# Where and when a mixture-of-experts kernel loads its router's logits, and the order of work around it

## The chip, the cores and the metric

The kernel runs on one core of a Trainium2 chip. The metric is the device time of one execution in microseconds; smaller is better. Times before: 385.84 us as the median of three runs (385.48 to 386.31). A core has TensorE (PE; matmuls, with its weight loads listed apart as PEld), VectorE (DVE), ScalarE (ACT), GpSimd (POOL) and SyncE (SP, which here only issues DMAs). TensorE writes its products to PSUM banks; the other data lie in SBUF. The engines run in parallel and wait for each other by semaphores; each engine takes its own instructions strictly in the order in which they were written.

## The reference

Two layers with residual connections, on x of shape (2, 1024, 256), with a condition of shape (2, 8):

```
rw = softmax(cond);  w, sel = top_k(rw, 2);  w = w / sum(w)          # two experts for each of the 2 batch rows
mlp(x, g, u, d) = (gelu_tanh(x @ g) * (x @ u)) @ d                   # 256 -> 1024 -> 256
x = x + sum_{s in sel} w_s * mlp(x, expert_s) + mlp(x, shared)       # 8 experts, one shared MLP
x = x + (x @ W_base.T + b_base + 2.0 * sum_e cond_e * (x @ A_e.T) @ B_e.T)
```

Of the 8 experts only the two chosen ones count for a batch row, so the kernel loads the weights of these two alone, by an index that it works out on the chip. For that it needs the 16 numbers of `cond_8` (the logits).

## The kernel before, in words

The work is cut into 24 groups: 2 batch rows, for each the shared MLP and two experts, for each 4 quarters of the 1024 inner columns (256 columns in two blocks of 128). `groups` at L185 lists them; groups 0 to 3 and 12 to 15 are the shared MLP's. A group's weights are one tile `w_raw` of 128 x 1536 numbers (768 KB): four blocks of the gate and up weights, A11, A12, A22, A21, and the down weights. Three such tiles turn round (`raw_ring`). Shared weights are loaded by SP; group 0's come in four pieces, between the four tiles of x (`load_first`, `load_x`). An expert's weights are gathered by GpSimd (`load_w`, L200), which needs the indices `idx`.

To keep float32 accuracy every operand is split into a high and a low part (`hi_of`, L179, and `lo_of`, L182), and a product of two blocks is three matmuls (high by high, low by high, high by low). The high parts are mostly made by ScalarE, the low parts by VectorE or GpSimd. A block in what follows is three matmuls of 128x128 by 128x512.

From group 1 on, the four 2 x 2 block products of the gate (g) and of the up weights (u) are computed by a scheme with seven products each, P1 to P7, in place of eight, with sums of the weight blocks (`weight_sum`, S1 to S4, made by GpSimd at L221 into `sf`) and of x (`x_sum`). The products gather in two PSUM banks for g and two for u, called a and d. In between, ScalarE copies what bank a holds to SBUF (`keep`, L310: r1 after P1, u2 after P6, u3 after P7), and VectorE adds that to bank d (`add_part`, L316: "r1 added", "u3 added", "u2 added"). The results are the four parts 00, 11, 10 and 01 of the hidden layer. Each then goes through gelu on ScalarE (L325), a product with the up part on VectorE (`times_up`, L331 and L333, "act 00" and so on), and a split into high and low part ("hi 00" on ScalarE, "lo 00" on VectorE). Then come six matmuls with the down weights into the banks y (L355), as two halves; the second half needs the low part. Group 0 does the same with eight plain products (`plain_product`, L306).

TensorE's order inside a group is thus a list of 14 blocks of products and 8 half-blocks of "down", 22 in all. All of it, for all engines, is one list: `at(t, f, ...)` at L106 puts a step with a due time t into `plan`, in units of about one block of TensorE, and L618 calls the steps in order of their due times. What a group repeats has its due time within the group in the table `REGULAR`, and group g adds g x 22 (`LEN`). `MOVED` shifts single steps by their number in the list. So a table of numbers sets the order in which each engine gets its instructions; nothing is reordered later. The waits follow from the data.

The parts that this change touches:

- `router_load` (L148) loads the logits to all 128 partitions (8 KB) and makes the row numbers by an iota on GpSimd. Its due time of 14.5 is shifted by `MOVED[11]` to -33.0, so it is the first step of all.
- `router` (L152, due 26) finds the two largest logits and the indices on VectorE. `gate_exp` and `gelu_table` (due 48.0 and 48.1, in group 2) run an exponential on ScalarE and then set the table for gelu again; `gate_weights` (due 52.5, L169 to L171) makes the experts' weights on VectorE. They are first used in group 4.
- SP's order at the start is: piece 0 of group 0's weights, x tile P1, piece 1, x tile P2, piece 2, x tiles B12 and P3, piece 3, the weights of group 1, of group 2, of group 3, the second layer's weights.

Of the kernel before, what the change touches and what calls it, by code (L numbers as in the profile page):

```python
# [50 lines left out]
P = 128  # L51
# [2 lines left out]
SCALING = 2.0  # L54
PIECE = 2
REGULAR = {
    "P1g": -3.3, "r1g": -2.5, "P2g": -0.5, "S1": -0.4, "A hi": -0.0, "P1u": 0.1, "r1u": 0.2,
    "r1 added g": 0.8, "P6g": 1.9, "u2g": 2.6, "P2u": 3.4, "gelu 00": 4.5, "P5g": 5.3, "S2": 5.5, "S4": 6.5,
    "P6u": 7.2, "load": 7.2, "S3": 7.9, "P7g": 8.4, "u2u": 8.7, "P5g mix": 9.0, "u3g": 9.7, "P7u": 11.3,
    "S hi": 12.0, "r1 added u": 12.1, "P5u": 12.2, "u3 added g": 12.7, "act 00": 12.7, "A1 lo": 13.4,  # L60
    "S lo": 13.5, "P4g": 13.8, "u3u": 14.1, "hi 00": 15.2, "gelu 11": 15.3, "P3g": 15.5, "u3 added u": 15.6,
    "act 11": 16.6, "gelu 10": 17.8, "P4u": 17.8, "u2 added g": 18.2, "P3u": 18.5, "hi 11": 19.4,
    "act 10": 19.7, "hi 10": 19.8, "lo 00": 20.7, "gelu 01": 21.2, "down 00 0": 21.3, "u2 added u": 21.7,
    "act 01": 22.9, "lo 11": 23.6, "down 00 1": 24.2, "A2 lo": 28.6, "hi 01": 29.5, "lo 10": 30.6,
    "down 11 0": 32.5, "down 11 1": 32.5, "down 10 0": 32.8, "D hi": 33.0, "lo 01": 33.2, "down 10 1": 33.3,
    "down 01 0": 34.0, "down 01 1": 35.1, "D1 lo": 36.1, "D0 lo": 36.3,
}
MOVED = {
    11: -47.5, 39: 2.3, 53: 0.6, 66: -0.2, 80: -1.0, 86: -11.0, 99: 7.4, 100: 6.6, 120: -2.6, 1577: 6.8,
    1580: 2.9, 1583: 6.7, 1604: 7.1,  # L70
}
WARM = 32
LEN = 22
# [15 lines left out]
def moe_then_lora(ctx: ExitStack, tc: tile.TileContext, x, cond, skill, shared, piece0, second, outT):  # L89

    nc = tc.nc
    B, T, NC, _, _ = x.shape
    E = cond.shape[1]
# [12 lines left out]
    def at(t, f, *args):  # L106
        plan.append((round(t + MOVED.get(len(plan), 0), 1), len(plan), f, args))
# [6 lines left out]
    def const(shape, dtype, name):  # L114
        return sb.tile(shape, dtype, name=name, tag=name)
# [22 lines left out]
    logits = const([P, B, E], F32, "logits")  # L138
# [7 lines left out]
    gate_w = const([P, TOP_K, B], F32, "gate_w")  # L146

    def router_load():  # L148
        nc.gpsimd.dma_start(out=logits, in_=bass.AP(cond.tensor, 0, [[0, P], [E, B], [1, E]]))
        nc.gpsimd.iota(row, pattern=[[1, NPC]], base=0, channel_multiplier=NPC)  # L150

    def router():  # L152
# [159 lines left out]
    sums, ge, act, acts = {}, {}, {}, {}  # L312
# [49 lines left out]
    mix, bias_sb = lin[:, (2 + NC) * C:(2 + NC) * C + B], lin[:, (2 + NC) * C + B:]  # L362
# [70 lines left out]
    V, A, G = nc.vector, nc.scalar, nc.gpsimd  # L433
# [8 lines left out]
    at(-29.4, load_x, 0, 1, 1)  # L442
    at(-29.3, load_first, 4 * G2, PW)
    at(-29.2, load_w, 1)
    at(14.5, router_load)
    at(17, load_w, 2)
    at(40, load_lora)

# [238 lines left out]
```

## Time and profile before

| What | us |
|---|---|
| median of three runs | 385.84 |
| the profiled execution, its own time | 386.39 |
| its span | 384.6 |
| one group of TensorE in the steady part (two runs of twelve down matmuls of the chain, 102.16 and 117.12) | 14.96 |
| TensorE busy in the first 10 us | 7.03 |
| TensorE busy from 40 to 50 us | 9.00 |
| VectorE busy from 155 to 170 us (about group 10) | 14.68 |
| VectorE busy from 245 to 260 us | 12.97 |
| GpSimd busy from 155 to 170 us | 9.44 |

The profile has a page of one execution and a trace that can be asked for more. In its lists a line of a wait reads: engine and line that waited, who released it, the sum, the times, the longest. A line of the order of time reads: start, duration, engine, line, operation, what is written and read. The granted TensorE clock is full over the whole span. All times inside the span are from its start. The names are the program's: `ps_ag` is bank a for the gate, `ps_du` bank d for the up weights, `acts` the split hidden parts, `xr` the loaded x tiles, `x` their split parts.

### The profile page before, as it was taken

How to read it: one execution, taken by the hardware profiler on the slowest of the kernel's cores; microseconds unless marked ns; L12 is line 12 of the kernel's file. 1: busy time of each engine (PE TensorE's matmuls, PEld its weight loads, DVE VectorE, ACT ScalarE, POOL GpSimd, SP SyncE). 2: the span in 40 equal slices, each digit the busy share in tenths (PEclk: the TensorE clock that was granted, in tenths of full speed). 3: DMA queues.
4: the chain of work that ended last, by engine and by line, in shares of the span. 5: the costliest groups of instructions: out<-in, count | busy, mean ns of one | idle time of the engine just before them, and what ended most of it. 6: DMA issues, size and time to landing. Idle time of an engine off the chain costs nothing.

```text
span 384.6 us, 4819 instructions
## 1 busy us (share of the span) xinstructions
PE 377.3 (98%) x1694; PEld 312.5 (81%) x1694; DVE 330.7 (86%) x421; ACT 250.8 (65%) x439; POOL 214.8 (56%) x216
## 2 busy tenths in 40 slices
PE   6999899999999999999999999999999999999996
PEld 5888788888888888888888888888888888888885
DVE  4999898697988999999989999889889889787586
ACT  3688786775775867757658767757667566575520
POOL 1676687689675574564463765755755745650100
PEclk9999999999999999999999999999999999999999
DMA  7611221120220213030342202202202112000014
GB/s 232 262 55 55 83 84 14 70 80 2 84 82 0 84 43 120 3 136 27 111 125 66 84 0 82 83 2 82 77 7 82 34 50 82 0 2 1 0 56 164
DMA packets 7831, 26.00 MB, mean 68 GB/s; under 512 B 880, under 2 KB 1664, under 8 KB 7808
## 3 DMA queue, kind: packets, MB, share of 16 engines
q0 software_dynamic: 2336, 12.59, 10.5%
q1 hardware_dynamic: 5472, 13.11, 9.9%
q8 instruction: 13, 0.21, 0.2%
q14 instruction: 10, 0.08, 0.1%
HBM read 23.60 MB, written 2.10 MB: 67 GB/s over the span
## 4 chain that ended last, share of the span: by engine, by line
PE 95%; ACT 2%; DMA 1%; DVE 1%; SPq 0%; issue 0%
PE y L355 33%; PE ps_au L286 17%; PE ps_ag L286 17%; PE ps_du L286 13%; PE ps_dg L286 13%; DMA xr<-in_x 1%; PE ps_dg L306 1%; PE ps_du L306 1%; PE ps_ag L306 1%; PE ps_au L306 1%; DVE gate_w L171 0%; PE ps_dg L378 0%; ACT L175 0%; ACT L165 0%; SPq L209 0%; ACT wa L179 0%
## 5 line engine op out<-in xcount | busy, mean ns | idle before, releaser
L355 PE MATMUL y<-acts,wd 128*128 128x512 f32 x576 | 149.9, 389 | 1.0 <-DVE acts L182 1.0
L355 PEld LDWEIGHTS y<-acts,wd 128*128 128x128 f32 x576 | 108.0, 188 | 23.8 <-DVE acts L182 1.4
L182 DVE TENSOR_TENSOR acts<-act,acts 128x512 fp32r<-128x512 f32 x96 | 90.5, 970 | 1.1 <-ACT acts L179 0.9
L182 POOL TENSOR_TENSOR wd<-w_raw,wd 128x256 fp32r<-128x256 f32 x44 | 41.9, 975 | 68.8 <-ACT wd L179 68.8
L182 POOL TENSOR_TENSOR wa<-w_raw,wa 128x512 fp32r<-128x512 f32 (+1 forms) x46 | 55.7, 1212 | 23.6 <-ACT wa L179 23.6
L179 ACT CAST acts<-act 128x512 fp32r<-128x512 f32 x96 | 59.6, 621 | 10.5 <-DVE act L331 6.4
L221 POOL TENSOR_TENSOR sf<-w_raw 128x256 f32<-128x256 f32 x46 | 44.6, 970 | 37.5 <-DVE ws L182 27.4
L310 ACT COPY u_u<-ps_au 128x512 f32<-128x512 f32 x46 | 27.1, 589 | 48.2 <-PE ps_au L286 48.1
L333 DVE SCALAR_TENSOR_TENSOR act<-ge,gate_w,c_u 128x512 f32<-128x512 f32 x48 | 46.4, 966 | 1.9 <-ACT ge L325 0.4
L316 DVE TENSOR_TENSOR c_u<-ps_du,u_u 128x512 f32<-128x512 f32 x46 | 31.4, 684 | 15.6 <-PE ps_du L286 12.8
L325 ACT ACTIVATE ge<-c_g 128x512 f32<-128x512 f32 x69 | 44.0, 638 | 0.0
L316 DVE TENSOR_TENSOR c_g<-ps_dg,u_g 128x512 f32<-128x512 f32 x46 | 31.6, 686 | 13.5 <-PE ps_dg L286 7.4
L286 PE MATMUL ps_au<-x,ws 128*128 128x512 f32 x138 | 38.8, 389 | 0.0
L286 PE MATMUL ps_ag<-x,ws 128*128 128x512 f32 x138 | 38.8, 389 | 0.0
L286 PE MATMUL ps_dg<-x,ws 128*128 128x512 f32 x138 | 38.8, 389 | 0.0
L286 PE MATMUL ps_du<-x,ws 128*128 128x512 f32 x138 | 38.8, 389 | 0.0
L286 PE MATMUL ps_ag<-x,wa 128*128 128x512 f32 x138 | 38.8, 389 | 0.0
L286 PE MATMUL ps_au<-x,wa 128*128 128x512 f32 x138 | 38.8, 389 | 0.0
L182 DVE TENSOR_TENSOR ws<-sf,ws 128x1024 fp32r<-128x1024 f32 (+1 forms) x24 | 37.2, 1552 | 0.0
L310 ACT COPY r_g<-ps_ag 128x512 f32<-128x512 f32 x23 | 13.5, 589 | 29.5 <-PE ps_ag L286 29.4
L286 PEld LDWEIGHTS ps_ag<-x,ws 128*128 128x128 f32 x138 | 25.9, 188 | 5.4
L286 PEld LDWEIGHTS ps_dg<-x,ws 128*128 128x128 f32 x138 | 25.9, 188 | 5.4
(102 smaller groups left out, 554.0 us busy)
## 6 DMA issues: line engine op xcount, KB each, us to landing
w_raw<-in_shared SPq DMA_DIRECT2D x7, 768.0 KB, 4.5
xr<-in_x SPq DMA_DIRECT2D x16, 256.0 KB, 2.9
lora_in<-in_second SPq DMA_DIRECT2D x1, 514.0 KB, 5.3
w_raw<-in_piece SPq DMA_DIRECT2D x2, 256.0 KB, 5.7
outT<-u_g SPq DMA_DIRECT2D x2, 256.0 KB, 2.0
outT<-u_u SPq DMA_DIRECT2D x2, 256.0 KB, 2.0
outT<-ge SPq DMA_DIRECT2D x4, 128.0 KB, 1.7
w_raw<-in_piece SPq DMA_DIRECT2D x2, 128.0 KB, 3.2
```

Source lines behind the costliest of these rows:

```text
L179: (eng.copy if eng is nc.scalar else eng.tensor_copy)(pair[:, 0, :], src)
L182: eng.tensor_tensor(pair[:, 1, :], src, pair[:, 0, :].bitcast(F32), ALU.subtract)
L221: eng.tensor_tensor(ssum(i), a, b, op)
L286: nc.tensor.matmul(ps, lhsT=l, rhs=r, start=(start and n == 0), stop=(n == len(parts) - 1), skip_group_check=True)
L306: nc.tensor.matmul(bank[plain_bank[ij], h], lhsT=w[:, wp, c:c + P], rhs=x[:, xp, :], start=(k == 0 and n == 0), stop=(n == 2), skip_group_ ...
L310: nc.scalar.copy(part[m, h], bank["a", h])
L316: nc.vector.tensor_tensor(sums[g, h, ij], bank["d", h], part[m, h], ALU.add)
L325: nc.scalar.activation(ge[g, ij], result(g, 0, ij), AF.Gelu_apprx_tanh)
L333: nc.vector.scalar_tensor_tensor(act[g, ij], ge[g, ij], gate_w[:, s - 1, b:b + 1], result(g, 1, ij), ALU.mult, ALU.mult)
L355: nc.tensor.matmul(y[j][c], lhsT=w[:, wp, o:o + P], rhs=a[:, ap, :], start=first and n == 0, stop=last and n == 2, skip_group_check=True)
```

## The change

The load of the logits is issued by SP, not by GpSimd, and its due time is -29.1: behind the weights of group 1 (-29.2) and ahead of those of group 2 (17). The iota stays on GpSimd. All due times in `REGULAR` are new, and so are the shifts in `MOVED`. For single steps: `x_sum(0,1)` (number 32) is done on VectorE between the high and the low part of x tile B12 and not behind the low part of group 0's down weights; the high part of P5 (40) goes ahead of group 0's gelu 10 on ScalarE; GpSimd's S3 of group 1 (86) keeps its place as GpSimd's first sum; gelu 11 of group 0 (74) goes ahead of the weight sums' split.

In the groups the order by due time changes as follows. Place 0 is P1g.

| place | TensorE before | TensorE after |
|---|---|---|
| 0 to 5 | P1g, down 00 first half, P2g, P1u, P6g, down 00 second half | the same |
| 6 to 9 | P2u, P5g, P6u, P7g | down 11 first half, P6u, P2u, P7g |
| 10 to 13 | down 11 first and second half, down 10 both halves | P5g, down 10 both halves, down 11 second half |
| 14 to 17 | P7u, down 01 first half, P5u, down 01 second half | the same |
| 18 to 21 | P4g, P3g, P4u, P3u | P3g, P4g, P4u, P3u |

On ScalarE "hi 10" moves from ahead of gelu 01 to behind the copy u2g, and the high part of the down weights and of the weight sums stand a little earlier. On VectorE "lo 10" goes ahead of "lo 11" (in groups 1 to 22); in group 2's stretch both stand ahead of `gate_weights`, where before `lo 10` stood behind it. On GpSimd, S3 goes ahead of the low part of A22 and of the gather, and the two low parts of the down weights change places.

```diff
--- before.py
+++ after.py
@@ -54,20 +54,20 @@
 SCALING = 2.0
 PIECE = 2
 REGULAR = {
-    "P1g": -3.3, "r1g": -2.5, "P2g": -0.5, "S1": -0.4, "A hi": -0.0, "P1u": 0.1, "r1u": 0.2,
-    "r1 added g": 0.8, "P6g": 1.9, "u2g": 2.6, "P2u": 3.4, "gelu 00": 4.5, "P5g": 5.3, "S2": 5.5, "S4": 6.5,
-    "P6u": 7.2, "load": 7.2, "S3": 7.9, "P7g": 8.4, "u2u": 8.7, "P5g mix": 9.0, "u3g": 9.7, "P7u": 11.3,
-    "S hi": 12.0, "r1 added u": 12.1, "P5u": 12.2, "u3 added g": 12.7, "act 00": 12.7, "A1 lo": 13.4,
-    "S lo": 13.5, "P4g": 13.8, "u3u": 14.1, "hi 00": 15.2, "gelu 11": 15.3, "P3g": 15.5, "u3 added u": 15.6,
-    "act 11": 16.6, "gelu 10": 17.8, "P4u": 17.8, "u2 added g": 18.2, "P3u": 18.5, "hi 11": 19.4,
-    "act 10": 19.7, "hi 10": 19.8, "lo 00": 20.7, "gelu 01": 21.2, "down 00 0": 21.3, "u2 added u": 21.7,
-    "act 01": 22.9, "lo 11": 23.6, "down 00 1": 24.2, "A2 lo": 28.6, "hi 01": 29.5, "lo 10": 30.6,
-    "down 11 0": 32.5, "down 11 1": 32.5, "down 10 0": 32.8, "D hi": 33.0, "lo 01": 33.2, "down 10 1": 33.3,
-    "down 01 0": 34.0, "down 01 1": 35.1, "D1 lo": 36.1, "D0 lo": 36.3,
+    "P1g": -2.2, "r1g": -1.4, "P2g": -1.3, "S1": -0.3, "A hi": -0.0, "r1 added g": 0.2, "P1u": 0.7,
+    "r1u": 0.7, "P6g": 1.7, "u2g": 2.1, "P6u": 4.6, "gelu 00": 5.2, "S2": 6.8, "S4": 6.8, "S3": 7.1,
+    "P2u": 7.4, "load": 7.4, "P7g": 7.8, "P5g mix": 8.6, "P5g": 8.7, "u2u": 8.8, "P7u": 10.2, "u3g": 10.6,
+    "S hi": 10.7, "r1 added u": 11.6, "A1 lo": 12.1, "u3 added g": 12.7, "act 00": 12.9, "P5u": 12.9,
+    "S lo": 14.3, "P3g": 14.4, "u3u": 14.5, "P4g": 14.9, "u3 added u": 16.2, "gelu 11": 16.3, "hi 00": 16.4,
+    "P4u": 16.4, "gelu 10": 16.7, "act 11": 16.8, "P3u": 17.8, "u2 added g": 18.0, "act 10": 18.6,
+    "hi 11": 19.6, "down 00 0": 20.3, "lo 00": 20.8, "gelu 01": 21.6, "u2 added u": 21.6, "act 01": 23.4,
+    "down 00 1": 25.0, "hi 10": 25.3, "down 11 0": 25.8, "lo 10": 28.4, "hi 01": 29.2, "A2 lo": 30.0,
+    "lo 11": 30.2, "down 10 0": 30.8, "down 10 1": 31.4, "down 11 1": 31.5, "D hi": 32.7, "lo 01": 32.9,
+    "down 01 0": 34.1, "down 01 1": 35.8, "D0 lo": 36.9, "D1 lo": 37.4,
 }
 MOVED = {
-    11: -47.5, 39: 2.3, 53: 0.6, 66: -0.2, 80: -1.0, 86: -11.0, 99: 7.4, 100: 6.6, 120: -2.6, 1577: 6.8,
-    1580: 2.9, 1583: 6.7, 1604: 7.1,
+    32: -9.6, 39: 0.8, 40: -5.4, 53: 0.9, 74: -2.1, 80: -1.3, 86: -42.5, 99: 7.1, 100: 6.3, 1514: -5.7,
+    1536: 3.7, 1577: 7.7, 1580: 3.3, 1583: 7.5, 1604: 8.8,
 }
 WARM = 32
 LEN = 22
@@ -146,7 +146,7 @@
     gate_w = const([P, TOP_K, B], F32, "gate_w")
 
     def router_load():
-        nc.gpsimd.dma_start(out=logits, in_=bass.AP(cond.tensor, 0, [[0, P], [E, B], [1, E]]))
+        nc.sync.dma_start(out=logits, in_=bass.AP(cond.tensor, 0, [[0, P], [E, B], [1, E]]))
         nc.gpsimd.iota(row, pattern=[[1, NPC]], base=0, channel_multiplier=NPC)
 
     def router():
@@ -442,7 +442,7 @@
     at(-29.4, load_x, 0, 1, 1)
     at(-29.3, load_first, 4 * G2, PW)
     at(-29.2, load_w, 1)
-    at(14.5, router_load)
+    at(-29.1, router_load)
     at(17, load_w, 2)
     at(40, load_lora)
```

## The prediction, made before the result was known

> **What bounds the kernel now.** I read the page first, then TensorE's waits, then the chain of work, then the first 8 us and the stretch from 36 to 43 us closely.
>
> ```profile
> PE 377.3 (98%) x1694; PEld 312.5 (81%) x1694; DVE 330.7 (86%) x421; ACT 250.8 (65%) x439; POOL 214.8 (56%) x216
> ...
> PE 95%; ACT 2%; DMA 1%; DVE 1%; SPq 0%; issue 0%
> ```
>
> TensorE is the bound: it works 377.3 of 384.6 us and carries 95% of the chain. The change adds and removes no matmul, so it can only win back idle time of TensorE, 7.3 us in all, or add some. TensorE's waits, with total, times and longest, show where the 7.3 us lie.
>
> ```profile
> PE ps_ag L306 <- DVE x L179: 2.2, 2, 1.6
> PE y L355 <- DVE acts L182: 1.0, 1, 1.0
> PE y L431 <- PEq L676: 0.8, 1, 0.8
> ```
>
> Out of reach are 0.8 us before the warm-up and the tail: the last matmul ends at 381.3, 3.3 us before the end, and the order of the last stores stays. In reach are 2.2 us at the start (0.6 ahead of the first product, 1.6 ahead of the second) and 1.0 us at 42 us. From 43 us to the tail no wait of TensorE is listed: there the change can only lose. The chain names what is late at the start (start, duration):
>
> ```profile
> 2.10 5.17 DMA xr<-in_x
> 7.28 0.02 issue
> 7.30 0.44 DVE x L179
> 7.74 0.14 issue
> 7.87 0.47 PE ps_ag L306
> ```
>
> The second x tile, issued at 2.10, lands at 7.27; the first, as large and issued at 1.17, is there by 4.07. In the table by stretch (the last two columns are DMA share and GB/s) one sees why:
>
> ```profile
> 3.00:3.50 0.50, 0.50 (x8) 0.50 (x7) 0.17 (x1) 0.30 (x1) 0.00 (x0) 1.00 0.85 319
> 3.50:4.00 0.50, 0.50 (x8) 0.36 (x6) 0.25 (x1) 0.00 (x0) 0.00 (x0) 1.00 1.35 147
> 4.00:4.50 0.50, 0.04 (x1) 0.00 (x0) 0.43 (x1) 0.00 (x0) 0.00 (x0) 1.00 0.67 41
> 4.50:5.00 0.50, 0.36 (x2) 0.35 (x3) 0.47 (x1) 0.00 (x0) 0.00 (x0) 1.00 1.10 45
> 5.00:5.50 0.50, 0.50 (x4) 0.41 (x3) 0.22 (x1) 0.00 (x0) 0.00 (x0) 1.00 0.59 215
> 5.50:6.00 0.50, 0.50 (x4) 0.29 (x2) 0.00 (x0) 0.09 (x1) 0.00 (x0) 1.00 0.77 283
> ```
>
> For a microsecond the DMA engines are busy and move almost nothing. The queue rows put the logits of GpSimd's queue (q0) in the same place: 26.0% of 16 engines from 3 to 4 us and 18.9% from 4 to 5, for 8 KB.
>
> **The change: the load.** GpSimd loses one issue of 0.73 us at 1.26. It then idles until 11.93, so that is worth 0. SP gets one issue, between those of group 1's and group 2's weights: 0.43 us by its neighbours, 0.73 us by GpSimd's row. All that SP has for the first TensorE stall is issued by then. Behind it stand the weights of groups 2 and 3 and the last layer's weights. Group 2's, issued at about 5.1 and landing 8.6 us later (13.7), come later by the issue plus the logits' transfer: 0.02 us by size at 400 GB/s, 1.3 us if they clog the engines again. At the worst they land at 15.8, and their first reader is GpSimd's L221 at 20.93. Group 3's wait for VectorE until 13.79 anyway. The logits land behind group 1's weights (11.9) and are read at 23.91. All this costs 0; the cover is 5 us or more.
>
> What it frees is the dip. Between 3.5 and 5.5 us 0.224 MB were moved (147, 41, 45 and 215 GB/s, half a microsecond each). At 283 GB/s it would have been 0.566 MB, so 0.34 MB are missing: 1.2 us at 283 GB/s, 0.85 us at the 400 GB/s of 7 us. Bounds: 0 if the dip is not the logits' doing, and 1.6 us at the top, where the first product's matmuls end. One rule of the Trainium skill speaks against a gain: by "DMA: Bandwidth & Descriptors", section "Queues, rings and completion order", a DMA engine takes its rings in turn and changes ring after each packet. Q0 has 32 packets, two for each engine, so a neighbour should lose two small packets, under 0.1 us, and the sum would be 0.1 instead of 1.1. The row says otherwise: 3.8% of 16 engines over the first 12 us is 7.3 us in 32 packets, 0.23 us each. I take **1.1 us**, by the row.
>
> To be kept, the gain needs VectorE, which is busy almost without a break from 7.3 to 23 us. It gets its inputs earlier by the same 1.1 us. `x_sum(0,1)` now stands ahead of B12's low part: that ends at 10.93 instead of 10.24 and is needed at 12.06. The same sum at its old place (L260, 13.72) took 1.78 us beside GpSimd, against 0.69 for its like at 10.76, so VectorE wins rather than loses by the move. The first down product needs group 0's low part of w_down at 15.2, and in the new order it is done at 14.5. In group 1, P6u goes two blocks (1.4 us) earlier, and its r1u copy ended 1.4 us ahead of it before; the copies move with the inputs. Price 0; without this cover up to 0.5 us.
>
> **The change: the stall at 42 us.** The chain of that stretch, by engine (start, duration):
>
> ```profile
> 36.76 1.28 ACT L165 ACT_TABLE_LOAD   x1
> 38.26 1.28 ACT L175 ACT_TABLE_LOAD   x1
> ```
> ```profile
> 36.96 1.22 DVE L182 TENSOR_TENSOR acts<-act,acts 128x512 fp32r<-128x512 f32 x1
> 39.79 0.27 DVE L169 TENSOR_SCALAR den<-ex 128x2 f32<-128x2 f32 x1 [1.60 <-ACT den L175]
> 40.30 1.80 DVE L171 TENSOR_TENSOR gate_w<-ex,gate_w 128x2 f32<-128x2 f32 x1
> 42.02 1.82 DVE L182 TENSOR_TENSOR acts<-act,acts 128x512 fp32r<-128x512 f32 x2
> ```
>
> ScalarE changes its table twice. VectorE waits 1.60 us for that, then spends 1.80 us on two numbers per partition, and only then makes the low part of block 10 (`lo 10`), for which TensorE waits 1.0 us. In the new order both `lo 10` and `lo 11` of group 1 stand ahead of the gate weights. `hi 10` goes on ScalarE between u2g (which ends at 36.74) and the tables, so the gate weights come 0.5 us later: den at 40.3, the product done by 41.0 (0.2 us) to 42.6 (1.80 again). `lo 10` runs at 37.2, `lo 11` until 39.5, both needed after 40.7. Queued behind the gate weights are `lo 01` (done by 43.2, needed at 44.3) and then r1 added u (done by 43.8), for which P5u waits at 43.4. So 0 to 0.5 us of stall stay where 1.0 was. The copy u2u, behind the tables on ScalarE, ends at 41.7 and P7u wants it at 42.0. Gain 0.5 to 1.0; I take **0.7 us**.
>
> **The change: the groups.** TensorE does one block in 0.68 us, 22 in a group (14.96 us). P5g goes 3 blocks later, P2u 2 later, P6u 1 earlier, half of `down 11` 4 earlier and half 2 later, `down 10` 1 earlier; P4g and P3g change places. I went through what each needs by the rows of the group from 125 us. VectorE's own order stays, but for `lo 10` and `lo 11`, which change places. The tightest links are these. P1g waits for gelu 10, which now starts 0.94 us after a P4g that is one block later: 0.5 us of slack, before 1.2. `lo 10` waits for `hi 10`, now behind u2g on ScalarE: `hi 10` ends at 144.8, VectorE comes to it at 145.2. In group 9 P6's high part now stands behind gelu 10, so act 10 comes 0.3 us later, with 0.84 us before P1u needs it. None reaches TensorE: price 0, bounds 0 to 1 us over the 23 groups.
>
> **Sum:** 1.1 + 0.7 = 1.8 us off the span of 384.6, which is 382.8; with the 1.8 us around it in the profiled execution (386.39) that is 384.6. That execution lies 0.55 us over the median, so against the median: 385.84 - 1.8 = **384.0 us**. Its own range: start 0.85 to 1.6, stall 0.5 to 1.0, so 383.2 to 384.5.
>
> **Rivals.** A measurement of this kernel tells about 0.2%, 0.77 us, from no change: faster is below 385.07, slower above 386.61.
> *The dip stays.* Bursts of DMA here often start badly: in the DMA view of 38 to 46 us the rate goes 123, 246, 61, 31, 154, 276 GB/s in slices of 0.2 us, with no logits about. Then the second x tile lands as before and only the 0.7 us remain: 385.1 (384.6 to 385.6). Against it: at 41 us the engines had been idle, at 4 us they had not.
> *VectorE holds the start.* If VectorE can't follow the earlier inputs, because GpSimd's sums also start earlier and slow it (L182's 128x512 takes 0.68 us alone, 1.2 to 1.8 beside GpSimd), half of the start's gain goes: 384.6. For it: it is busy there without a break; against: it gets its own inputs earlier too. I count it, with 0.1 of the first case's 0.50, at that case's upper end.
> *Slower: VectorE waits in its queue in groups 8 to 11.* There it is busy for 13.9 to 14.7 us of 15 (other groups 13), so it can give up about 0.4 us a group. If `hi 10` or P6's high part comes later than I reckon by w, everything behind waits, and TensorE with it once the slack of 0.5 to 0.9 us is used up: 4 (w - 0.4) us. It decides from w = 1.0 (2.4 us lost against 1.8 won), and with w = 1.3 the time is 385.84 - 1.8 + 3.6 = 387.6. For it: VectorE has no spare wait there. Against: its order is nearly the same.
>
> **How the numbers follow.** First case 0.50, dip stays 0.27, slower mechanism 0.23. Faster: 0.50 and half of the second case, 0.13, is 0.63. Same: the other half, 0.14, and 0.03 of the third, 0.17. Slower: 0.20. The range reaches from 383.0 (the first case with all bounds at their best, a little over) to 387.3, which leaves out about 0.13 of the third case and 0.05 below.
>
> **What would show it.** Right: no dip between 4 and 5 us, the second x tile landing by 6.4, the second product at 6.8 instead of 7.87; the wait of `y` for `acts` at 42 us gone or below 0.5; no new wait of TensorE after 45 us. The forecast is wrong if the dip is there without q0, if TensorE's waits list a link of the groups several times, or if VectorE's share in groups 8 to 11 reaches 15 of 15.

## The result, and the profile after

The changed kernel takes 384.96 us (median of 8 runs, 383.72 to 385.45), the kernel before beside it on the same chip 386.04 us (8 runs, 385.48 to 386.31). The ratio is 0.997, with a 95% interval of 0.9957 to 0.9982: 1.1 us faster. The forecast was 384.0, with its own range 383.2 to 384.5 and the full range 383.0 to 387.3. So the sign is right, the time lies in the full range, and the gain is some 60% of the 1.8 us that the sum gave. It lies outside the first case's own range, and inside the range of the rival "the dip stays" (384.6 to 385.6), although the dip went. A second set of 22 runs gave 385.14 us and a ratio of 0.9976 (0.9968 to 0.9983).

The profiled execution is the slowest of the eight: its own time is 385.45 us and its span 383.6 us, against 386.39 and 384.6 before. The page of the changed kernel, busy times and chain by engine:

```profile
PE 378.0 (99%) x1694; PEld 313.0 (82%) x1694; DVE 324.8 (85%) x421; ACT 252.1 (66%) x439; POOL 210.7 (55%) x215
...
PE 95%; DMA 1%; DVE 1%; ACT 1%; SPq 0%; issue 0%
```

TensorE has the same 1694 matmuls and is still the bound. GpSimd has one issue less. The whole list of TensorE's waits (total, times, longest):

```profile
PE ps_ag L306 <- DVE x L179: 1.2, 1, 1.2
PE y L431 <- PEq L676: 0.8, 1, 0.8
PE ps_du L286 <- DVE c_u L316: 0.3, 1, 0.3
```

No link of the groups is in it. The wait of `y` for `acts` is gone, and P5u (`ps_du` for `c_u`) waits 0.34 us in its place. Of the 2.2 us at the start 1.2 are still there. The stretches of half a microsecond between 3.5 and 6 us (the last two columns are DMA share and GB/s) and the chain there (start, duration):

```profile
3.50:4.00 0.50, 0.50 (x7) 0.50 (x6) 0.46 (x2) 0.00 (x0) 0.00 (x0) 1.00 0.70 248
4.00:4.50 0.50, 0.42 (x5) 0.19 (x2) 0.47 (x2) 0.33 (x1) 0.00 (x0) 1.00 1.41 221
4.50:5.00 0.50, 0.50 (x2) 0.40 (x3) 0.50 (x2) 0.07 (x1) 0.00 (x0) 1.00 0.63 180
5.00:5.50 0.50, 0.50 (x4) 0.41 (x3) 0.32 (x1) 0.00 (x0) 0.00 (x0) 1.00 0.93 234
5.50:6.00 0.50, 0.50 (x4) 0.32 (x2) 0.00 (x0) 0.00 (x0) 0.00 (x0) 1.00 1.17 217
```
```profile
2.10 4.86 DMA xr<-in_x
...
6.98 0.44 DVE x L179
...
7.55 0.47 PE ps_ag L306
```

The dip of 41 and 45 GB/s is filled: 221 and 180 GB/s. Yet the second x tile lands after 4.86 us where it took 5.17, and the second product starts at 7.55, not at 6.8 as forecast, where it was 7.87. The bytes flowed; the tile was hardly earlier.

At 42 us, VectorE's order of time, then GpSimd's and TensorE's rows of the same stretch:

```profile
36.89 1.89 DVE L182 TENSOR_TENSOR acts<-act,acts 128x512 fp32r<-128x512 f32 x2 [0.40 <-ACT acts L179]
39.91 1.98 DVE L169 TENSOR_SCALAR den<-ex 128x2 f32<-128x2 f32 x1 [1.13 <-ACT den L175]
41.93 0.17 DVE L170 RECIPROCAL gate_w<-den 128x2 f32<-128x2 f32 x1
42.12 0.16 DVE L171 TENSOR_TENSOR gate_w<-ex,gate_w 128x2 f32<-128x2 f32 x1
42.20 0.68 DVE L182 TENSOR_TENSOR acts<-act,acts 128x512 fp32r<-128x512 f32 x1
42.80 0.68 DVE L316 TENSOR_TENSOR c_u<-ps_du,r_u 128x512 f32<-128x512 f32 x1
```
```profile
39.86 1.99 POOL L182 TENSOR_TENSOR wa<-w_raw,wa 128x256 fp32r<-128x256 f32 x2
```
```profile
43.54 0.74 PE L286 MATMUL ps_du<-x,ws 128*128 128x512 f32 x2 [0.34 <-DVE c_u L316]
```

Both low parts of row 1 now run at 36.89, ahead of the gate weights, and nothing waits for them. The gate weights still cost VectorE 2.3 us: this time it is L169, not L171, that spends 1.98 us on two numbers per partition. What is late next is `r1 added u` (L316), and P5u with it.

The marks on TensorE say how the profiled pair's gain is divided. The second product is 0.32 us earlier, P1g of group 1 starts at 18.55 for 18.87, also 0.32, and at 42 us 0.66 comes in (1.0 less 0.34): 0.98 together. The last row of matmuls starts at 379.53 for 380.44, 0.91 earlier.

### The profile page after: what moved, and what is told of

The parts are those of the page before. It is cut to its first block, busy times and chain, and to the rows that moved or that the text cites. A ratio compares the mean times of both kernels' runs of the same rounds, so it can differ in the third digit from the quotient of the medians.

```text
span 383.6 us, 4881 instructions
## 1 busy us (share of the span) xinstructions
PE 378.0 (99%) x1694; PEld 313.0 (82%) x1694; DVE 324.8 (85%) x421; ACT 252.1 (66%) x439; POOL 210.7 (55%) x215
## 4 chain that ended last, share of the span: by engine, by line
PE 95%; DMA 1%; DVE 1%; ACT 1%; SPq 0%; issue 0%
PE y L355 33%; PE ps_ag L286 17%; PE ps_au L286 17%; PE ps_du L286 13%; PE ps_dg L286 13%; DMA xr<-in_x 1%; PE ps_dg L306 1%; PE ps_du L306 1%; PE ps_ag L306 1%; PE ps_au L306 1%; DVE den L169 1%; PE ps_dg L378 0%; ACT L175 0%; ACT L165 0%; SPq L209 0%; DVE acts L182 0%
## 5 line engine op out<-in xcount | busy, mean ns | idle before, releaser
L182 DVE TENSOR_TENSOR acts<-act,acts 128x512 fp32r<-128x512 f32 x96 | 74.3, 805 | 5.6 <-ACT acts L179 3.9
L221 POOL TENSOR_TENSOR sf<-w_raw 128x256 f32<-128x256 f32 x46 | 41.7, 906 | 35.7 <-DVE ws L182 25.2
L333 DVE SCALAR_TENSOR_TENSOR act<-ge,gate_w,c_u 128x512 f32<-128x512 f32 x48 | 54.4, 1132 | 1.7
L316 DVE TENSOR_TENSOR c_u<-ps_du,u_u 128x512 f32<-128x512 f32 x46 | 31.4, 684 | 14.7 <-PE ps_du L286 12.4
L325 ACT ACTIVATE ge<-ps_ag 128x512 f32<-128x512 f32 x25 | 14.9, 597 | 38.7 <-PE ps_ag L286 38.0
L316 DVE TENSOR_TENSOR c_g<-ps_dg,u_g 128x512 f32<-128x512 f32 x46 | 31.5, 684 | 7.6 <-PE ps_dg L286 7.2
L310 ACT COPY u_g<-ps_ag 128x512 f32<-128x512 f32 x46 | 27.0, 587 | 13.8 <-PE ps_ag L286 11.8
L286 PEld LDWEIGHTS ps_du<-x,ws 128*128 128x128 f32 x138 | 25.8, 188 | 6.1 <-DVE c_u L316 0.8
```

The costliest lines, as they stand in the source:

```text
L182: eng.tensor_tensor(pair[:, 1, :], src, pair[:, 0, :].bitcast(F32), ALU.subtract)
L221: eng.tensor_tensor(ssum(i), a, b, op)
L286: nc.tensor.matmul(ps, lhsT=l, rhs=r, start=(start and n == 0), stop=(n == len(parts) - 1), skip_group_check=True)
L310: nc.scalar.copy(part[m, h], bank["a", h])
L316: nc.vector.tensor_tensor(sums[g, h, ij], bank["d", h], part[m, h], ALU.add)
L325: nc.scalar.activation(ge[g, ij], result(g, 0, ij), AF.Gelu_apprx_tanh)
```

## The experiments

Each was timed in five rounds beside the kernel before. A ratio is formed from all runs, so that a few late ones move it more than the median. The kernel before had a median of 386.24 us beside the first four, 386.18 beside the next four and 386.10 beside the last two.

**The changed kernel once more**, as the measure for the others.

> The changed kernel once more, beside the others on one chip: 0.3% faster than before (385.0 against 386.0), as in its first comparison. In its profile the second product starts at 7.3 to 7.6 us (7.55 in the first profile), and P5u waits about 0.3 us at 43 us. If the start varies by itself from one execution to the next, the second x tile lands anywhere between 6 and 7 us.

Measured: 385.14 us (384.49 to 386.31). Its second product starts at 7.16, earlier than the 7.3 to 7.6 expected, its first P1g at 18.16; P5u waits 0.4. The second x tile lands at 6.56, so the start does vary by itself.

**The load alone**: the order before, with the load on SP behind group 1's weights.

```diff
-        nc.gpsimd.dma_start(out=logits, ...)
+        nc.sync.dma_start(out=logits, ...)
 MOVED:
-    11: -47.5,
+    11: -43.6,
```

> The old order of work, with only the logits' load moved to SP behind group 1's weights. Theory A (the load slowed the start, the order of work mends the stall at 42 us): 0.3 to 0.5 us faster than before, second product at 7.4 to 7.6 instead of 7.87, and the wait of y for acts at 42 us stays at 1.0 us. Theory B (the load made no difference, all the gain is the new order): no difference, 0.0 us, second product where it was. My forecast's reckoning (1.1 us from the load) would give 1.1 us and a second product at 6.8.

Measured: 385.78 us (384.95 to 388.52), ratio 0.9994 (0.998 to 1.0009): not told from no change. TensorE's waits:

```profile
PE y L355 <- DVE acts L182: 1.1, 1, 1.1
PE y L431 <- PEq L676: 0.8, 1, 0.8
PE ps_ag L306 <- DVE x L179: 0.6, 1, 0.6
PE ps_du L306 <- DVE act L331: 0.3, 1, 0.3
```

The second product starts at 6.40, without a wait: the start's gain is there in full, 1.47 us against before. The first down product starts at 13.36 instead of 14.78. Then a wait that is in neither kernel (`ps_du` for `act`, at 15.44) takes half of it back. It is listed with 0.3 us of idle time, but the matmuls on both sides of it lie further apart too, and from start to start it costs 0.6. P1g of group 1 starts at 18.10, and of the 1.47 us 0.77 are left. VectorE ahead of that wait, in order of time:

```profile
11.25 0.68 DVE L182 TENSOR_TENSOR acts<-act,acts 128x512 fp32r<-128x512 f32 x1
11.85 1.23 DVE L182 TENSOR_TENSOR wd<-w_raw,wd 128x512 fp32r<-128x512 f32 x1
13.01 1.77 DVE L260 TENSOR_TENSOR xr<-xr,xr 128x512 f32<-128x512 f32 x1
14.71 0.68 DVE L331 TENSOR_TENSOR act<-ge,ps_du 128x512 f32<-128x512 f32 x1
```

The sum of x tiles at L260 takes 1.77 us ahead of act 10, for which TensorE waits. In the new order the same sum, `x_sum(0,1)`, takes 0.68 at another place:

```profile
9.07 0.68 DVE L260 TENSOR_TENSOR xr<-xr,xr 128x512 f32<-128x512 f32 x1
```

So in the old order VectorE holds the start, and by these rows the sum that the change moves is in its way.

**The order alone**: the changed kernel with the load first on GpSimd's queue, as before.

```diff
-        nc.sync.dma_start(out=logits, ...)
+        nc.gpsimd.dma_start(out=logits, ...)
-    at(-29.1, router_load)
+    at(-33.0, router_load)
```

> The new order of work, with the logits' load still first on GpSimd's queue. Theory A: 0.6 to 0.7 us faster than before (0.2%), the wait at 42 us down from 1.0 to 0.3, second product at 7.8 to 7.9. Theory B: the whole gain of the change, 1.0 us.

Measured: 385.64 us (385.03 to 387.85), ratio 0.9994 (0.998 to 1.0008). The second product is at 7.89, as before the change; the wait at 42 us is down to P5u's 0.3. By medians the load alone gives 0.46, the order alone 0.60, together 1.06, and the changed kernel 1.10 (386.24 to 385.14). Each half lies within the uncertainty of its own measurement; the whole doesn't.

**The gate weights alone**: before, with the gate weights one step later, behind lo 10.

```diff
-    at(2 * LEN + 8.5, gate_weights)
+    at(2 * LEN + 8.7, gate_weights)
```

> The kernel before, with one edit: the gate weights stand behind lo 10 in VectorE's order. If the stall at 42 us is that queue alone, the wait of y for acts (1.0 us) goes and the kernel is 0.7 to 1.0 us faster than before, as much as the new order gives or more, since no wait of P5u for r1 added u need take its place (in the old order P5u comes at the same place, so 0 to 0.3 us may come back). If the new order's gain at that place came from something else, the wait stays or moves and the gain is below 0.3 us.

Measured: 385.27 us (384.34 to 387.01), ratio 0.9982 (0.9971 to 0.9993). TensorE's waits:

```profile
PE ps_ag L306 <- DVE x L179: 0.9, 2, 0.7
PE y L431 <- PEq L676: 0.8, 1, 0.8
```

At 42 us no wait is listed at all. P1g of group 3 lies 15.30 us behind P1g of group 2, where it was 16.29 before: 0.99 of stall gone, 0.3 more than the change itself wins there. This one due time has nearly the gain of the whole change.

**Is it the queue, or the time?** The old order, with the load on GpSimd's queue as before, but behind GpSimd's first sum (issued at 12.14).

```diff
 MOVED:
-    11: -47.5,
+    11: -7.4,
```

> The kernel before, with the logits still on GpSimd's queue but issued behind GpSimd's first sum, at about 13 us. If it is the place in time and not the queue that counts, this does to the start what SP's queue does: no small packets before 12 us, the second x tile at 5.8 to 7.0 us, 0.3 to 0.5 us faster than before. If it is the queue (GpSimd's own way of issuing), it gains as well, so this run tells only against a gain of SP's queue itself: equal to e1_load_only within 0.3 us is what both the time and my theory say; slower than e1_load_only by over 0.5 us would mean that SP's queue has a merit of its own.

Measured: 386.07 us (385.31 to 387.38), ratio 1.0008 (0.9996 to 1.0021). The second product is at 6.22, as early as with SP: what counts is that the load is not among the first transfers, not which queue issues it. P1g of group 1 is at 18.35. Act 10 holds TensorE again (0.4 us), and no time is won where 0.3 to 0.5 us were expected.

**The load later still on SP**: the changed kernel, with the load behind group 2's weights.

```diff
-    at(-29.1, router_load)
+    at(17.1, router_load)
```

> The changed kernel with the logits' load one place later on SP, behind group 2's weights (issued at about 5.7, read at the earliest at 12 us). The slow packets of 0.3 to 1.9 us between 4 and 7.5 us, which the changed kernel still has, are there without any logits if they belong to the x tiles and weights themselves: second x tile at 5.8 to 7.0 us, same time as the changed kernel within 0.3 us. If the logits still did harm at their place in SP's queue, the slow packets would be gone, the second x tile would land by 5.5 us, and it would be 0.5 to 1.0 us faster than the changed kernel.

Measured: 385.04 us (383.94 to 386.23), ratio 0.9971 (0.9959 to 0.9984), the same as the changed kernel. Its profiled run is its fastest. There the second product follows the first at once:

```profile
5.56 0.40 PE L306 MATMUL ps_au<-x,wa 128*128 128x512 f32 x1
5.87 0.47 PE L306 MATMUL ps_ag<-x,wa 128*128 128x512 f32 x1
```

This one execution, at 383.94, has the forecast's time, and wins more at the start than the forecast had: its second product is 2.0 us earlier than before.

**The gate weights later in the changed kernel**, behind lo 01 and `r1 added u`.

```diff
-    at(2 * LEN + 8.5, gate_weights)
+    at(2 * LEN + 11.7, gate_weights)
```

> The changed kernel with the gate weights moved on VectorE behind lo 01 and r1 added u. The rest of the stall at 42 us, P5u's wait of 0.3 to 0.4 us for r1 added u, goes: 0.3 us faster than the changed kernel, 384.8 where that one is 385.1. If something else stood behind it (the part of VectorE's order after the gate weights is late too), a wait of 0.1 to 0.3 us comes up at P3g or P3u and nothing is gained.

Measured: 384.76 us (384.37 to 385.14), ratio 0.9968 (0.9957 to 0.9979); its median lies 0.2 or 0.4 under the changed kernel's two, but the intervals overlap. P5u's wait is gone from the list:

```profile
PE y L431 <- PEq L676: 0.8, 1, 0.8
PE ps_ag L306 <- DVE x L179: 0.4, 2, 0.2
```

Yet P1g of group 3 comes 15.57 us behind P1g of group 2, where it was 15.64 in the changed kernel: 0.07 us are won there, not 0.3. P5u and two blocks behind it, P3g and P3u, take 0.94 to 0.96 us each where the others take 0.85, and P3g and P3u start 0.1 and 0.2 us late. The list, which has idle time only, does not show it. The rows of P3g and P3u:

```profile
43.96 0.96 PE L286 MATMUL ps_dg<-x,ws 128*128 128x512 f32 x3
46.30 0.96 PE L286 MATMUL ps_du<-x,ws 128*128 128x512 f32 x3
```

So by the profile the expectation's other case came true: a delay at P3g and P3u, and nothing gained. What makes the median lower isn't shown; it may be the scatter of the start.

**The first two x tiles on ScalarE's queue**, on top of that, so that the second is issued 0.9 us earlier. The table of gelu is set behind these issues.

```diff
-        nc.sync.dma_start(out=xraw[b, k, j], in_=x[b, j, k])
+        (nc.scalar if (b, j) == (0, 0) else nc.sync).dma_start(out=xraw[b, k, j], in_=x[b, j, k])
-    at(-30, gelu_table)
+    at(-29.6, gelu_table)
```

> e6_gate_later with the first two x tiles issued by ScalarE ahead of its table load, so that the issues of 0.43 us on SP no longer follow each other: the second x tile is issued at about 1.2 instead of 2.1. If the issue order sets the landing, it lands about 0.9 us earlier (by 5.5 to 6.1), the second product follows the first without a wait, and the time is 0.5 to 1.0 us below e6_gate_later. If slow packets of single DMA engines set it, it lands at 6 to 7 us as before and the time is that of e6_gate_later, within 0.3 us; slower is possible, since the first gelu table comes 0.9 us later.

Measured: 384.24 us (384.04 to 386.36), ratio 0.9958 (0.9945 to 0.997), the best of the runs. The second x tile, issued at 1.16, lands at 4.93, earlier than the 5.5 to 6.1 expected and than in any profile with the tiles on SP's queue. Whether the earlier issue does this or the other queue wasn't separated. Ten of its twelve times lie between 384.04 and 384.87, two at 386.28 and 386.36. The profiled one is 386.28, and TensorE's order of time there shows why:

```profile
0.76 3.57 PE L431 MATMUL y<-const-bfloat16-1.0 128*128 128x128 bf16 x32 [0.76 <-PEq L676]
5.10 0.77 PE L306 MATMUL ps_ag<-x,wa 128*128 128x512 f32 x1 [0.77 <-ACT wa L179]
5.67 0.63 PE L306 MATMUL ps_au<-x,wa 128*128 128x512 f32 x1
6.09 0.63 PE L306 MATMUL ps_ag<-x,wa 128*128 128x512 f32 x1
...
8.65 0.63 PE L306 MATMUL ps_ag<-x,wa 128*128 128x512 f32 x1
9.08 0.58 PE L306 MATMUL ps_au<-x,wa 128*128 128x512 f32 x1
9.50 0.39 PE L306 MATMUL ps_ag<-x,wa 128*128 128x512 f32 x1
```

After the warm-up TensorE pauses for 0.8 us. Then ten matmuls follow each other at 0.43 us instead of 0.23, which is 2 us. The trace's first record of the granted clock, at full speed, stands at 9.47 us, where the pace changes.

**A longer warm-up**, on the last two kernels (44 and 40 matmuls).

```diff
-WARM = 32
+WARM = 44
```

> The version with the first two x tiles on ScalarE's queue and the gate weights last (384.24 us), with 44 matmuls of warm-up instead of 32, so that TensorE has no pause between the warm-up, which ended at 4.33, and the first product at 5.1. Theory A (TensorE falls back to half pace when it pauses at about 4.3 us; the ten first matmuls followed each other at 0.43 us instead of 0.23, which is 2 us): the first matmuls follow each other at 0.23 us in the profile, no run lies 2 us above the others, median 383.9 to 384.3. Theory B (the half pace has to do with what the weights or inputs find, not with the pause): matmuls at 0.43 us from 5.1 as before, some runs at 386.3, median 384.2 or above.

> The changed kernel with the gate weights last (384.76 us), with 40 matmuls of warm-up instead of 32; otherwise unchanged. There the first six matmuls of the first product took 0.43, 0.43, 0.37, 0.23, 0.23 us from one to the next after a pause of 0.23 us. Theory A: all at 0.23 us, and 0.3 to 0.6 us less time: 384.2 to 384.5. Theory B, or the second x tile, at 6.4, is the later wait anyway so that the pace of the first product doesn't count: 384.6 to 384.9, and the wait of the second product grows by what the first wins.

Measured with 44 and the tiles on ScalarE's queue: 384.50 us (384.11 to 385.10, 6 runs), ratio 0.9964 (0.9951 to 0.9976). No run of the six is at 386, and the pace is the full one from the first matmul on:

```profile
0.76 4.01 PE L431 MATMUL y<-const-bfloat16-1.0 128*128 128x128 bf16 x44 [0.76 <-PEq L676]
5.07 0.47 PE L306 MATMUL ps_ag<-x,wa 128*128 128x512 f32 x1 [0.30 <-DVE x L179]
5.38 0.40 PE L306 MATMUL ps_au<-x,wa 128*128 128x512 f32 x1
5.62 0.40 PE L306 MATMUL ps_ag<-x,wa 128*128 128x512 f32 x1
```

The median is not better than with 32, so the warm-up removes the lost 2 us where they fall and adds nothing elsewhere. With two late runs of twelve before, of which one was profiled, six runs without one could also be chance; the pace in the profile is the stronger evidence. The second x tile lands at 4.90 here.

With 40 and the tiles on SP's queue: 385.15 us (384.14 to 385.48), ratio 0.9971 (0.9959 to 0.9983), no better than 384.76 with 32. The first product runs at 0.23 us per matmul there too, but the second x tile's cast came at 6.88 and TensorE waited 0.96 us for it. What the pace wins the second tile takes, as the second theory has it, though the time lies above what either theory gave. It is also a second measure of the kernel with the gate weights last, 0.4 us slower than the first.

## Why the prediction was right in sign and too large

**The stall at 42 us** was forecast at 0.7 (0.5 to 1.0) and measured at 0.66, with the remainder at P5u as the prediction named it. The long instruction was not the one it named: the product (L171) took 0.16 us, the short one of its two cases, and L169 ahead of it took 1.98. The end of the gate weights lay in the forecast all the same (42.28, forecast 41.0 to 42.6), in part by luck.

**The groups at nothing**: right. No wait is listed after 43.54, and the slower rival, a queue on VectorE in groups 8 to 11, has no row.

**The cost of the moved load at nothing**: right. SP issued it at 4.95 in 0.70 us, nearer to GpSimd's 0.73 than to its neighbours' 0.43 (0.46 in the load later still). The load later still made no difference to the time.

**The start at 1.1 us** is the step that failed: it brought 0.32 us in the profiled pair, and 0.5 to 0.7 us as worked out below. The prediction took the bytes missing in the dip, divided by the rate of the whole core. The dip did vanish, but TensorE waits for the last part of a tile. The trace records the landing of each load in 16 parts. Before, those of the second x tile came between 5.99 and 7.28 us. After the change thirteen came between 4.46 and 5.60, and the last three at 6.87, 6.88 and 6.95, and the cast for which TensorE waits starts at 6.98. So the first part gained 1.5 us and the last 0.33. The packets show it too: one of 2 KB (an x tile's or a weight piece's) takes 0.084 us as a rule, but three that began at 4.2 us took 1.7 to 1.9 us, and others that began between 5 and 6 us up to 1.2, while the rest flowed. Why single packets are so slow stays open. The rival "the dip stays" named the reason, that bursts here often start badly, though the dip did not stay as it had it.

How much the load does for the landing can be seen over the ten profiles that have these tiles on SP's queue. They differ in the first 19 us only by order, load and warm-up. Landing of the second x tile (half of its parts, and all), start of the second product, and of P1g of group 1:

| kernel | order | load | tile in: half, all | second product | P1g | between |
|---|---|---|---|---|---|---|
| before | old | first, GpSimd | 6.42, 7.28 | 7.87 | 18.87 | 11.00 |
| gate weights alone | old | first, GpSimd | 5.87, 7.00 | 7.60 | 18.59 | 10.99 |
| order alone | new | first, GpSimd | 5.78, 7.29 | 7.89 | 18.88 | 10.99 |
| load alone | old | later, SP | 5.33, 5.80 | 6.40 | 18.10 | 11.70 |
| GpSimd, late | old | later, GpSimd | 4.94, 5.62 | 6.22 | 18.35 | 12.13 |
| changed | new | later, SP | 4.96, 6.95 | 7.55 | 18.55 | 11.00 |
| changed again | new | later, SP | 4.87, 6.56 | 7.16 | 18.16 | 11.00 |
| load later still | new | later, SP | 4.75, 5.28 | 5.87 | 16.92 | 11.05 |
| gate weights later | new | later, SP | 4.84, 6.35 | 6.95 | 17.93 | 10.98 |
| the same, 40 warm-up | new | later, SP | 5.66, 6.86 | 7.46 | 18.44 | 10.98 |

With the load first the mean of the second product is 7.79, with it later 6.80: 0.99 us earlier, close to the 1.1 of the sum, but scattered over 5.9 to 7.6 where it was 7.6 to 7.9. So the logits do delay the second tile. The rule of the Trainium skill that was weighed in the prediction does not cover this: eight of the 16 packets of 512 B took 0.55 to 1.21 us in the trace of before, where the prediction made it under 0.1 us for two packets. The other slow packets remain and decide, run by run, how much of the gain arrives.

In time the load is worth less: 0.50 us in the new order (385.64 against 385.14, measured side by side). The choice of the profiled executions explains a good part of the gap to 0.99. There is one for each kernel; that of the load later still is the fastest of its twelve runs, that of the changed kernel the slowest of its eight. In the six kernels of the new order the span less the start of P1g is 365.0 to 365.3 us, so what differs between their executions is mostly the start. Moving each second product by the distance of its profiled run from its kernel's median gives an estimate of 6.96 to 7.37 (mean 7.12) with the load later, and of 7.79 with it first: 0.67 us. The half pace after the warm-up (below) doesn't account for the small gain in the profiled run of the changed kernel: its first product was through at 6.3 and TensorE waited for the tile.

The order alone is worth 0.6, near the 0.66 at 42 us. So the measured 1.1 is made of this and of 0.5 for the load, where the sum had 0.7 and 1.1. That the time still fell into the full range is owed to the width of that range, not to this term.

The last column answers the prediction's other rival. In the new order what the start wins reaches P1g nearly whole in all six. In the old order a win of 1.5 us loses 0.7 to VectorE with the load alone; with GpSimd late 1.1 are lost, some 0.6 of them to VectorE and 0.4 at `ps_dg`, which waits for ScalarE. "VectorE holds the start" is wrong for the kernel as changed and right without the change of order: the sentence that VectorE "wins rather than loses by the move" of `x_sum(0,1)` carried more than the prediction gave it. That this sum is the reason is read from the rows; it wasn't moved alone.

## What to carry to other kernels

A stretch without bytes on the DMA engines is not yet time to be won: a tile is there with its last part, so estimate from landings of the same tile in several profiles rather than from bytes over the mean rate. Keep small loads that nobody needs soon out of the first burst, on whatever queue, and see that the vector engine's order can use the earlier start; otherwise it comes back as a wait some microseconds later. Before reordering hundreds of due times, look at the listed waits one by one: here one step moved by one place gave nearly the whole gain.

## What the runs showed of the hardware

**TensorE's pace after the warm-up.** Where the 32 warm-up matmuls took 3.28 to 3.54 us (before, load alone, GpSimd late), the first product ran at 0.23 us per matmul despite a pause of up to 0.63 us. Where they took 3.57 us, all of them at half pace (0.107 us each, not 0.058), the first matmuls behind them came 0.4 us or more apart: one after a pause of up to 0.15 us (the changed kernel, once more, load later still), two or three after 0.2 us, ten after 0.77. The Trainium skill, "TensorE: Matmul & The Clock Gate", Part 1 on the clock gate, has it that a gate sets half or full clock by TensorE's activity in windows of about 3.4 us that run free of the kernel's start, with 0.427 us per matmul of 512 columns at half clock. That fits: a warm-up just as long as a window leaves it to chance whether a window closes as a busy one before the pause. The runs with 40 and 44 agree, at full pace from the first product on.

The trace agrees as well. Its records of the granted clock begin with full speed at 3.55 us before, 4.97 in the changed kernel, 6.15 with the order alone and 9.47 in the run that lost 2 us, each time where the pace of the matmuls changes. For the stretch ahead there is no record, and the row of the page shows it as full clock. So the clock is not full over the whole span: by the pace it is half up to 3.55 us before the change and up to 4.97 us after it.

**A vector instruction on two numbers per partition** took 1.80 us (L171, before) or 1.98 us (L169, after). The other one took 0.27 and 0.16 us there, and with the gate weights last, beside GpSimd's split of `wd`, the two take 0.36 and 0.46 us. The rows of GpSimd at 40.77 in the kernel before, and of VectorE and GpSimd with the gate weights last:

```profile
40.77 1.30 POOL L182 TENSOR_TENSOR wa<-w_raw,wa 128x512 fp32r<-128x512 f32 x1
```
```profile
42.26 0.36 DVE L169 TENSOR_SCALAR den<-ex 128x2 f32<-128x2 f32 x1
42.65 0.17 DVE L170 RECIPROCAL gate_w<-den 128x2 f32<-128x2 f32 x1
42.85 0.46 DVE L171 TENSOR_TENSOR gate_w<-ex,gate_w 128x2 f32<-128x2 f32 x1
```
```profile
41.85 1.44 POOL L182 TENSOR_TENSOR wd<-w_raw,wd 128x256 fp32r<-128x256 f32 x2 [0.67 <-ACT wd L179]
```

GpSimd's split ends at 42.07 and the long L171 of before at 42.10; with the gate weights last the splits end at 42.59 and 43.29, L169 and L171 at 42.62 and 43.31. In all twelve traces each L169 or L171 that took more than 0.17 us ended within 0.04 us of the end of a GpSimd instruction, so its length goes with what GpSimd still had to do. The reciprocal, L170, took 0.17 us beside GpSimd too. Why it is free of this, and why the longest ones outlast one GpSimd instruction and end with the next, stays open.

**The same load on two queues.** The logits' 8 KB are 16 packets of 512 B on GpSimd's queue and 128 of 64 B on SP's. In the first burst those of 512 B took up to 1.21 us (before), at 14 us up to 0.37 (GpSimd late); those of 64 B on SP's queue never took more than 0.02.
